# A gated recurrence on one core: the state in quarters of the columns by 32 of the batch, all products in 32-column tiles

## The chip, the core and the metric

The kernel runs on one core of a Trainium2 chip. The metric is the device time of one execution in microseconds (us), as the median of several runs. The core has TensorE (PE: products, with a separate weight load, PEld, before each), VectorE (DVE), ScalarE (ACT), GpSimd (POOL) and SyncE (SP, which issues most DMAs). Each engine works through its own queue in order, and semaphores tie the queues together. Products are written to PSUM, which has 128 partitions.

## What is computed

A gated recurrent unit over x of 64 sequences, 128 steps and 512 columns, all f32, with the input added to its output. The reference, cut to what matters:

```python
def step(h, inp):
    x_t, prop = inp
    comb = jnp.concatenate([x_t, h], axis=-1)
    z = jax.nn.sigmoid(comb @ Wz + bz)
    r = jax.nn.sigmoid(comb @ Wr + br)
    comb2 = jnp.concatenate([x_t, r * h], axis=-1)
    h_cand = jnp.tanh(comb2 @ Wh + bh)
    h_new = (1.0 - z) * h + z * h_cand
    h_next = jnp.where(prop, jnp.tanh(h_new @ Wp + bp), h_new)
    return (h_next, h_new)
# out = x + all h_new; prop is true at every fourth step but the last
```

Wz, Wr and Wh have 1024 rows: the first 512 meet x, the last 512 meet the state (or r * h). Wp has 512 rows. The order of the steps is forced; the products with x can be made ahead.

## The kernel before

**State.** `h`, `rh`, `z` and `keep` are tiles of 128 partitions by 256 columns (N): the 64 sequences (B) with the left half of the 512 columns lie on partitions 0 to 63, with the right half on 64 to 127.

**Products.** The transposed state is the weight of a product and a row block of W streams past it. `products` issues one call for each half of W's columns, with 64 columns of weight each; the output start (partition 0 or 64) puts the two into two 64-column tiles of TensorE. Each f32 call leaves two weight loads and two products in the trace (two passes). A gate is four such `products`, one for each 128 rows of W: 16 records of 128x256. All have line 225 in the profile.

**Turns.** The state must be transposed before it can be a weight. `turn` does 128 columns at a time on TensorE, as bf16 words against an identity (line 248, four records), and copies the result out of PSUM by VectorE or ScalarE (line 239). A state takes two `turn`s, eight records.

**A step** `t` (from line 677): the R gate on `hT`; sigmoid by ScalarE (line 751) and the product with h by VectorE (line 752), each in two halves of the columns; most of the Z gate, and in it the turns of `rh`; the two sigmoids of Z (lines 775, 776) and `keep` (line 777); the H gate on `rhT`; tanh (line 808), multiply (line 809) and add (line 814) in two halves; the turns of `h`, the first copied by VectorE, the second by ScalarE. In every fourth step ("Wp step") another gate with Wp, tanh (line 836) and turns of `hprop` follow. `seed` (line 410) copies the part of a gate that comes from x into PSUM before the products add the rest.

**The products with x.** For the first four and the last two steps they are plain. For all others, groups of four steps are done by a scheme with fewer multiplications: sums of blocks of x (GpSimd), sums of blocks of W (once), 192-column products into four PSUM banks `scratch_q`, `_r`, `_a`, `_x`, and sums back (`end_1`, `end_2`, lines 539 to 550: copies by ScalarE, adds by VectorE; then GpSimd, lines 580 and 584) into `cp`, from which `seed` reads. A unit of this work is one `products` call, four records. `batches` lists 98 units for eight steps; they stand in a list `queue`, and `fill(n)` puts the next n units where a step says. `read_out` issues the `end_` group of units that have been placed. How many go where is written out by hand in `PLACES`, three counts for each of eight steps, and in `TAIL` for the last nine. So TensorE's order is fixed in the program. x arrives twice, as `xr` (state layout, for the final sum) and as `xs` (for the transposed x, which VectorE makes with its own transpose, line 281).

Before the first step, `idle` issues products of zeros.

Of the kernel before, what the change touches and what calls it, by code (L numbers as in the profile page):

```python
# [17 lines left out]
def kernel(  # L18
# [14 lines left out]

# [5 lines left out]
    N = H // S  # L53
    C = N // P
# [6 lines left out]
    assert B * S == P and D == H and T % 8 == 0  # L61
# [10 lines left out]
    zeros = one.tile([P, 2 * N], BF16, tag="cq", name="zeros")  # L72
    nc.vector.memset(zeros, 0.0)
    ident = const.tile([P, P], F32, name="ident")
    make_identity(nc, ident)
    ones = const.tile([1, B], F32, name="ones")
    nc.gpsimd.memset(ones, 1.0)
    ident16 = const.tile([P, P], BF16, name="ident16")
    nc.vector.tensor_copy(ident16, ident)

# [5 lines left out]
    tw = {n: const.tile([P, S, S, 3, P], F32, name=f"tw_{n}") for n in (2, 3, 4)}  # L86
    tt = const.tile([P, 7, 3, S, 3, P // 2], F32, name="tt")
# [5 lines left out]
    def load_x(tile_, t0, n, j=0):  # L93
        for s in range(S):
            nc.sync.dma_start(
                out=tile_[s * B : (s + 1) * B, j : j + n, :], in_=x[:, t0 : t0 + n, ts(s, N)]
            )

    def load_w(wt, w, k0, k1, eng):
        eng.dma_start(  # L100
            out=wt[:, k0:k1, :],
            in_=w[k0 * P : k1 * P, :].rearrange("(k p) n -> p k n", p=P),
        )

    ORDER = [s * C + c for c in range(C) for s in range(S)]
    xr = {}

    def new_xr(g):
        xr[g] = xrp.tile([P, Q4, N], F32, tag="xr", name=f"xr_{g}")

    h_init = two.tile([P, N], F32, tag="h", name="h_init")
    bias_in = const.tile([P, 4, N], F32, name="bias")
    new_xr(0)
    for s in range(S):
        (nc.sync, nc.scalar)[s].dma_start(  # L115
            out=xr[0][s * B : (s + 1) * B, 0:2, :], in_=x[:, 0:2, ts(s, N)]
        )
    for k in ORDER:
        load_w(wx[:, :, R, :], Wr, k, k + 1, nc.sync)
    for i in (Z, H_):  # L120
        for k in (0, 2):
            load_w(wx[:, :, i, :], gates_in[i], k, k + 2, nc.sync)

    def load_bias(i, eng):
        for s in range(S):
            eng.dma_start(
                out=bias_in[s * B : (s + 1) * B, i, :],
                in_=(br, bz, bh, bp)[i][ts(s, N)]
                .rearrange("(o n) -> o n", o=1)
                .broadcast_to([B, N]),  # L130
            )
# [6 lines left out]
    for s in range(S):  # L138
        nc.gpsimd.dma_start(out=h_init[s * B : (s + 1) * B, :], in_=h0[:, ts(s, N)])
    for i in range(3):  # L140
        for k in (0, 2):
            load_w(wh[i], gates_in[i][D:, :], k, k + 2, nc.sync)
        if i == 0:
            load_x(xr[0], 2, 2, 2)
# [4 lines left out]

    xs = {}  # L150

    def load_xs(g):
        if g * Q4 < T:
            xs[g] = one.tile([P, Q4, S * C, 2, 32], F32, tag=f"xs{g % 2}", name=f"xs_{g}")
            for r in range(4):
                for bh in range(2):
                    nc.sync.dma_start(  # L157
                        out=xs[g][ts(r, 32), :, :, bh, :].rearrange("p t k e -> p (t k) e"),
                        in_=x[ts(bh, 32), g * Q4 : (g + 1) * Q4, :].rearrange(
                            "b t (k r e) -> r b (t k) e", k=S * C, r=4  # L160
                        )[r],
                    )

    load_xs(1)
    load_xs(2)
    load_w(wp, Wp, 0, 4, nc.sync)
    load_bias(3, nc.sync)
    new_xr(1)
    load_x(xr[1], 4, 4)


    rc = ps_c.tile([P, 2, N], F32, name="rc")
    zp = ps_c.tile([P, 2, N], F32, name="zp")
    slots = (rc[:, 0, :], zp[:, 0, :], rc[:, 1, :])
    slot_p = zp[:, 1, :]
    scratch = [ps_c.tile([P, 2 * N], F32, name=f"scratch_{n}") for n in "qrax"]
    q_ps, r_ps, a_ps, x_ps = (
        s[:, : 6 * P // 2].rearrange("p (m g u) -> p m g u", m=2, g=3) for s in scratch
    )


    turn_ps = [ps_c.tile([P, 2 * N], F32, name=f"turn_{c}") for c in range(C)]
    act_ps = [ps[:, N : N + P] for ps in turn_ps]

# [3 lines left out]
    def cut(ps):  # L188
        return ps.rearrange("p (c n) -> p c n", c=C)

    def spread(bank, rows, which):

        bank = bank.rearrange("p (i n) -> p i n", i=2)
        n = len(which)
        for s in range(S):
            nc.tensor.matmul(
                bank[s * B : (s + 1) * B, 0:n, :],
                lhsT=ones,
                rhs=bias_row[:, rows, ts(s, N)],
                start=True,  # L200
                stop=True,
            )
        for j, i in enumerate(which):
            nc.scalar.copy(bias_in[:, i, :], bank[:, j, :])

    bias0 = bias[:, 0, 0:3, :]
    bias_d = const.tile([P, 3, P], F32, name="bias_d")


    def idle(n):  # L210
        for i in range(n):
            s = i % S
            nc.tensor.matmul(
                (rc, zp)[i // S % 2][s * B : (s + 1) * B, :, :],
                lhsT=zeros[:, :B],
                rhs=zeros,
                start=True,
                stop=True,
            )


    def products(ps, lhs, rhs, start=False):

        for s in range(S):
            nc.tensor.matmul(  # L225
                ps[s * B : (s + 1) * B],
                lhsT=lhs,
                rhs=rhs(s),
# [4 lines left out]

    def product(ps, lT, w, k, start=False):
        s0, c0 = divmod(k, C)
        products(ps, lT[:, c0, ts(s0, B)], lambda s: w[:, k, ts(s, N)], start)

    def copy(eng, dst, src):
        (eng.copy if eng is nc.scalar else eng.tensor_copy)(dst, src)  # L239

    def turn(src, dst, c, name, eng):


        pt = turn_ps[c][:, :P].bitcast(BF16).rearrange("p (w n) -> p w n", w=2)
        for s in range(S):
            words = src[:, c * P + s * B : c * P + (s + 1) * B].bitcast(BF16)
            for w in range(2):
                nc.tensor.transpose(  # L248
                    pt[s * B : (s + 1) * B, w, :],
                    words.rearrange("p (n w) -> p w n", w=2)[:, w, :],  # L250
                    ident16,
                )
        copy(
            eng,
            dst[:, c, :].bitcast(U16).rearrange("p (n w) -> p n w", w=2),
            pt.bitcast(U16).rearrange("p w n -> p n w"),
        )

    def new_T(tag, name):
        return two.tile([P, C, P], F32, tag=tag, name=name)  # L260

# [3 lines left out]
    def new_xT(g):  # L265
        if g not in xT:
            xT[g] = xtp.tile([P, Q4, C, P], F32, tag="xT", name=f"xT_{g}")

    def turn_x(t, eng=nc.scalar):
        g, i = divmod(t, Q4)  # L270
        new_xT(g)
        src = xr[g]
        for c in range(C):
            turn(src[:, i, :], xT[g][:, i], c, f"xT_{t}", eng)

    def join_x(g, i):

        if g * Q4 >= T:
            return
        new_xT(g)  # L280
        nc.vector.transpose(  # L281
            out=xT[g][:, i].rearrange("p c (s b) -> p s c b", s=S),
            in_=xs[g][:, i].rearrange("p (s c) h e -> p s c (h e)", s=S),
        )


    def outer(kb, nb, ka):

        return wx[:, ka * C + kb, :, :].rearrange("p g (s n u) -> p n s g u", s=S, n=C)[:, nb]

# [11 lines left out]
    def inner(i, ka, na):  # L302
        return OPERAND[i](ka)[:, :, :, ts(na, P // 2)]

    def factor(i, j):

# [27 lines left out]

# [67 lines left out]
    def new_cp(q):  # L402
        if q not in cp:
            cp[q] = one.tile([P, C, 2, 3, P], F32, tag=f"cp{q % 2}", name=f"cp_{q}")
# [3 lines left out]
    def seed(i, t):  # L408
        if t < T:
            nc.scalar.copy(cut(slots[i]), G[t][:, :, i, :])  # L410

# [14 lines left out]

    def plain(t):

        first, second = scratch[:2] if t % 2 == 0 else scratch[2:]
        regions = (first[:, :N], first[:, N:], second[:, :N])  # L430
        g, i = divmod(t, Q4)

        def end():
            new_cp(t // 2)
            nc.vector.tensor_add(  # L435
                G[t][:, :, 0:2, :],
                first.rearrange("p (g c n) -> p c g n", g=2, c=C),
                bias[:, :, 0:2, :],
            )
            nc.vector.tensor_add(G[t][:, :, 2, :], cut(second[:, :N]), bias[:, :, 2, :])  # L440


        order = [(e, k) for e in range(3) for k in ORDER]
        if t == Q4 - 1:
            order = [(e, k) for k in ORDER for e in range(3)]
        units = [
            lambda e=e, k=k: product(
                regions[e], xT[g][:, i], wx[:, :, e, :], k, k == ORDER[0] and e != Z
# [3 lines left out]
        return [(u, None) for u in units[:-1]] + [(units[-1], end)]  # L452

    def plain_last():


        def banks(t):
            return scratch[:2] if t % 2 == 0 else scratch[2:]

        def units(t, gates, ks):  # L460
            first, second = banks(t)
            regions = (first[:, :N], first[:, N:], second[:, :N])
            return [
                lambda e=e, k=k: product(
                    regions[e], xT[LAST][:, t % Q4], wx[:, :, e, :], k, k == 3 and e != Z
# [5 lines left out]
        def end(t, gates):  # L471
# [485 lines left out]
```

## Time and profile before

| what | value |
|---|---|
| time, median of 3 runs | 1329.24 us (1328.91 to 1330.4) |
| profiled execution, first to last instruction | 1328.5 us, 37,727 instructions |
| mean granted TensorE clock | 0.999 |
| TensorE products / weight loads | 1319.2 us (99%) / 1117.0 us (84%), 15,312 each |
| VectorE / ScalarE / GpSimd | 57% / 42% / 66% |
| DMA | 62.22 MB, 171,438 packets, 133,600 of them under 512 bytes |

The profile is of one execution of its own; its time is given as the span in the second row, and nothing around that span is recorded. In a group's row stand the line, engine, operation, output<-input by name, shapes and count, then busy time and mean duration in ns, then idle time before it and what ended that. Durations of products overlap, so their count times their mean is more than their busy time; what they cost is read from start to start.

### The profile page before, as it was taken

What the parts mean: (1) busy time and instruction counts of PE and PEld (TensorE: products, weight loads), DVE (VectorE), ACT (ScalarE), POOL (GpSimd) and SP (SyncE); (2) the same over time, 40 slices, a digit from 0 to 9 for tenths busy, and PEclk for the clock granted to TensorE, in tenths of its full rate; (3) what the DMA queues carried; (4) which work ended last, traced back from release to release, by engine and by line L of the source; (5) the groups of instructions that cost most, each with busy time, mean ns of one, the idle gap of its engine ahead of it and who ended that gap; (6) DMA issues with size and microseconds to landing.
All of it is one profiled execution on the core that took longest, in us unless ns stands there. A gap on an engine that the chain in (4) does not pass through costs nothing.

```text
span 1328.5 us, 37727 instructions
## 1 busy us (share of the span) xinstructions
PE 1319.2 (99%) x15312; PEld 1117.0 (84%) x15312; DVE 750.8 (57%) x2000; ACT 554.4 (42%) x1733; POOL 881.5 (66%) x1032
## 2 busy tenths in 40 slices
PE   9999999999999999999999999999999999999998
PEld 5888888888888888888888888888888888888865
DVE  3655555555555555555555555555555555555544
ACT  1344444444444444444444444444444444444433
POOL 4876766766767577675777757676676676757530
PEclk9999999999999999999999999999999999999999
DMA  8421122121121221222111221212212112121030
GB/s 236 90 50 30 21 49 49 33 49 34 33 49 33 54 45 18 49 43 56 33 33 34 50 49 34 47 20 49 49 34 49 34 33 49 33 49 33 18 104 17
DMA packets 171438, 62.22 MB, mean 47 GB/s; under 512 B 133600, under 2 KB 166496, under 8 KB 171264
## 3 DMA queue, kind: packets, MB, share of 16 engines
q1 hardware_dynamic: 170880, 59.47, 20.8%
q8 instruction: 121, 1.98, 0.6%
q14 instruction: 53, 0.43, 0.1%
q10 hardware_dynamic: 224, 0.20, 0.1%
q0 software_dynamic: 160, 0.14, 0.0%
HBM read 43.00 MB, written 16.78 MB: 45 GB/s over the span
## 4 chain that ended last, share of the span: by engine, by line
PE 96%; SPq 1%; DMA 1%; DVE 0%; issue 0%; ACT 0%; DVEq 0%; ACTq 0%
PE rc L225 33%; PE zp L225 20%; PE scratch_q L225 11%; PE scratch_r L225 11%; PE scratch_x L225 11%; PE scratch_a L225 5%; PE turn L248 5%; DMA xr<-in_x_dram 1%; SPq L157 1%; SPq L100 0%; DMA bias<-in_L_cond_bp_dram 0%; DVE wx L333 0%; DVE turn L809 0%; SPq L115 0%; DVE xT L281 0%
## 5 line engine op out<-in xcount | busy, mean ns | idle before, releaser
L225 PE MATMUL rc<-wh,rhT 128*64 128x256 f32 x2048 | 246.0, 379 | 0.0
L580 POOL TENSOR_TENSOR cp<-mb,mb 128x768 f32<-128x768 f32 x75 | 136.3, 1818 | 107.4 <-ACT rc L410 47.5
L225 PE MATMUL zp<-wh,hT 128*64 128x256 f32 x1536 | 204.6, 379 | 0.0
L225 PEld LDWEIGHTS rc<-wh,rhT 128*64 128x64 f32 x2048 | 168.6, 137 | 40.1
L225 PE MATMUL rc<-wh,hT 128*64 128x256 f32 x1536 | 186.5, 383 | 0.4
L891 POOL TENSOR_TENSOR xr<-xr,h 128x256 f32<-128x256 f32 x127 | 92.7, 730 | 126.3 <-DVE h L814 126.3
L225 PEld LDWEIGHTS rc<-wh,hT 128*64 128x64 f32 x1536 | 122.3, 137 | 36.1 <-issue 10.1
L580 POOL TENSOR_TENSOR cp<-mb 128x768 f32<-128x768 f32 x47 | 85.3, 1815 | 94.7 <-DVE h L814 89.8
L225 PEld LDWEIGHTS zp<-wh,hT 128*64 128x64 f32 x1536 | 119.7, 137 | 24.7
L809 DVE TENSOR_TENSOR turn<-turn,z 128x128 f32<-128x128 f32 x256 | 75.4, 295 | 102.2 <-ACT turn L808 100.7
L239 DVE COPY rhT<-turn 128x256 uint16<-128x256 uint16 x256 | 97.6, 420 | 56.0 <-PE turn L248 51.6
L751 ACT ACTIVATE turn<-rc 128x128 f32<-128x128 f32 x256 | 55.3, 260 | 171.4 <-issue 113.8
L239 ACT COPY hT<-turn 128x256 uint16<-128x256 uint16 x127 | 47.3, 373 | 165.5 <-DVE hT L239 130.7
L548 DVE TENSOR_TENSOR mb<-scratch_r,cq 128x384 f32<-128x384 f32 (+1 forms) x107 | 59.3, 554 | 91.8 <-ACT cq L547 90.3
L580 POOL TENSOR_TENSOR mb<-mb,mb 128x768 f32<-128x768 f32 x58 | 105.4, 1817 | 8.5 <-DVE mb L550 8.5
L541 DVE TENSOR_TENSOR cx<-scratch_r,cx 128x384 f32<-128x384 f32 (+1 forms) x107 | 59.3, 554 | 88.0 <-ACT cx L539 88.0
L775 ACT ACTIVATE z<-zp 128x256 f32<-128x256 f32 x128 | 49.2, 384 | 136.7 <-PE zp L225 136.7
L410 ACT COPY rc<-cp 128x256 f32<-128x256 f32 x256 | 96.4, 377 | 18.3 <-DVE cp L435 4.6
L808 ACT ACTIVATE turn<-rc 128x128 f32<-128x128 f32 x256 | 55.2, 260 | 112.8 <-PE rc L225 111.7
L814 DVE TENSOR_TENSOR h<-turn,keep 128x128 f32<-128x128 f32 x254 | 74.1, 292 | 15.2
L248 PEld LDWEIGHTS <-h 128*64 128x64 bf16 x1016 | 68.1, 110 | 12.2 <-DVE h L814 6.5
L248 PE MATMUL turn<-ident,h 128*64 128x128 bf16 x1016 | 77.8, 220 | 0.3 <-DVE h L814 0.3
(165 smaller groups left out, 2931.7 us busy)
## 6 DMA issues: line engine op xcount, KB each, us to landing
xs<-in_x_dram SPq DMA_DIRECT2D x248, 64.0 KB, 2.8
xr<-in_x_dram SPq DMA_DIRECT2D x62, 256.0 KB, 4.1
out_dram<-xr SPq DMA_DIRECT2D x62, 256.0 KB, 3.3
wx<-in_L_cond_Wr_dram SPq DMA_DIRECT2D x7, 256.0 KB, 4.5
wx<-in_L_cond_Wz_dram SPq DMA_DIRECT2D x2, 512.0 KB, 6.4
wx<-in_L_cond_Wh_dram SPq DMA_DIRECT2D x2, 512.0 KB, 9.5
wh<-in_L_cond_Wr_dram SPq DMA_DIRECT2D x2, 512.0 KB, 12.7
wh<-in_L_cond_Wz_dram SPq DMA_DIRECT2D x2, 512.0 KB, 13.0
```

The lines of the kernel that those rows point to most:

```text
L225: nc.tensor.matmul(ps[s * B : (s + 1) * B], lhsT=lhs, rhs=rhs(s), start=start, stop=True, skip_group_check=True,)
L239: (eng.copy if eng is nc.scalar else eng.tensor_copy)(dst, src)
L248: nc.tensor.transpose(pt[s * B : (s + 1) * B, w, :], words.rearrange("p (n w) -> p w n", w=2)[:, w, :], ident16,)
L410: nc.scalar.copy(cut(slots[i]), G[t][:, :, i, :])
L541: nc.vector.tensor_add(T2[n][:, :nm], r_ps[:, :nm], T2[n][:, :nm])
L548: nc.vector.tensor_add(blocks()[:, :nm, 0, 1], r_ps[:, :nm], q2[:, :nm])
L580: nc.gpsimd.tensor_add(dst, a, b)
L751: nc.scalar.activation(act_ps[c], slots[R][:, ts(c, P)], AF.Sigmoid)
L808: nc.scalar.activation(pc, slots[H_][:, ts(c, P)], AF.Tanh)
L809: nc.vector.tensor_mul(pc, pc, z[:, ts(c, P)])
L814: nc.vector.tensor_add(h_new[:, ts(c, P)], pc, keep[:, ts(c, P)])
L891: nc.gpsimd.tensor_add(xr[g][:, j, :], xr[g][:, j, :], h_new)
```

## The change

The state is cut once more: quarters of the columns (J = 128) by 32 sequences (V). Partitions 32q to 32q+31 hold quarter q for one half of the batch, and the two halves of the batch lie side by side in the free dimension, [128, 2, 128]. With this layout the transpose that a product needs is one of 32x32 squares, which VectorE does in one instruction for a half. `product` and `products` now issue one call for each quarter of W's columns and each half of the batch: weights of 32 columns in four tiles, streams of 128 columns in a gate and of 96 in the batches.

```diff
+    def turn(dst, src):
+        nc.vector.transpose(out=dst, in_=src)
     def products(ps, lhs, rhs, start=False):
-        for s in range(S):
+        for q in range(NQ):
             nc.tensor.matmul(
-                ps[s * B : (s + 1) * B],
+                ps[part(q)],
                 lhsT=lhs,
-                rhs=rhs(s),
+                rhs=rhs(q),
...
+    def gate(i, lT, w):
+        for h in range(S):
+            for k in range(K):
+                products(
+                    pair(i)[:, h, :], lT[:, h, ts(k, V)], lambda q: w[:, k, ts(q, J)]
+                )
```

A step is now two chains, one for each half of the batch. The turns stand in VectorE's queue right behind what makes the state, and none stands in TensorE's:

```diff
+        gate(R, hT, wh[R])
...
+        for half in range(S):
+            r = pair(R)[:, half, :]
+            nc.scalar.activation(r, r, AF.Sigmoid)
+            nc.vector.tensor_mul(rh[:, half, :], r, h[:, half, :])
+            turn(rhT[:, half, :], rh[:, half, :])
...
+        gate(Z, hT, wh[Z])
...
+        fill(places[0])
+        gate(H_, rhT, wh[H_])
         read_out()
...
+        for half in range(S):
+            c = pair(H_)[:, half, :]
+            nc.scalar.activation(c, c, AF.Tanh)
+            nc.vector.tensor_mul(c, c, z[:, half, :])
...
+            nc.vector.tensor_add(h_new[:, half, :], c, keep[:, half, :])
+            turn(hT[:, half, :], h_new[:, half, :])
...
+        fill(places[1])
...
         if prop:
+            gate(P_, hT, wp)
             read_out()
+            for half in range(S):
+                nc.scalar.activation(h[:, half, :], pair(P_)[:, half, :], AF.Tanh)
+                turn(hT[:, half, :], h[:, half, :])
+            fill(places[2])
```

The hand-written places follow, 98 units for eight steps as before; the Wp steps are the first and the fifth of a row:

```diff
     PLACES = (
-        (6, 8, 6), (1, 7), (6, 6), (1, 7), (6, 8, 6), (1, 7), (1, 7), (6, 8),
+        (8, 3, 0), (3, 8, 0), (6, 8, 0), (6, 8, 0), (6, 4, 0), (4, 6, 0), (8, 6, 0), (8, 6, 0),
     )
```

Besides: the four PSUM banks `rc`, `zp` and `turn_0/1` become one tile `rec` of four banks, in which the two halves of R, of H and of the Wp gate lie in two different banks and Z in one; the x part, the sums of blocks and the batch products go to the same layout, with operands of the same number of elements for GpSimd, ScalarE and VectorE; x comes in eight transfers for each group and use, in rows of 512 bytes, and the outputs leave in eight for four steps (before: two and eight in, two out); the transposed x of the first eight steps is made from `xr`, so one `xs` load falls away; the weights come in transfers of 256 KB; the last output of each half leaves as soon as it is made, one on SP's queue and one on ScalarE's; `idle` issues 64, 16 and 32 products where it issued 16, 4 and 8; some of GpSimd's sums move by a step.

## The prediction

> **What bounds the kernel now.** I read the busy line of the page first, then the chain that ended last, then equal stretches, then TensorE in order of time, then groups by shape.
>
> ```profile
> PE 1319.2 (99%) x15312; PEld 1117.0 (84%) x15312; DVE 750.8 (57%) x2000; ACT 554.4 (42%) x1733; POOL 881.5 (66%) x1032
> PEclk9999999999999999999999999999999999999999
> PE 96%; SPq 1%; DMA 1%; DVE 0%; issue 0%; ACT 0%; DVEq 0%; ACTq 0%
> ```
>
> TensorE is busy 99% at the full granted clock, and the chain is 96% TensorE. A busy TensorE need not be a saturated one, so I looked at how its products stand in time. Two stretches of eight steps each:
>
> ```profile
> core 0: us, PE busy (x) PEld busy (x) DVE busy (x) ACT busy (x) POOL busy (x), PEclk, DMA share, GB/s
> 132.17:213.38 81.21, 81.21 (x954) 70.15 (x953) 46.92 (x125) 34.95 (x111) 56.21 (x67) 1.00 0.19 41
> 213.38:294.59 81.21, 81.21 (x955) 70.11 (x954) 46.92 (x125) 34.95 (x111) 56.24 (x67) 1.00 0.20 41
> ```
>
> The period is 81.21 us twice, without a hole. One step of it, columns start, length, engine, line, count:
>
> ```profile
> 133.76 1.49 PE L225 MATMUL zp<-wh,hT 128*64 128x256 f32 x12
> 135.05 0.42 PE L248 MATMUL turn<-ident,rh 128*64 128x128 bf16 x8
> 135.28 0.63 PE L225 MATMUL zp<-wh,hT 128*64 128x256 f32 x4
> 135.71 0.52 PE L225 MATMUL scratch_x<-tt,o 128*64 128x192 f32 x4
> 136.04 1.93 PE L225 MATMUL rc<-wh,rhT 128*64 128x256 f32 x16
> 137.76 0.53 PE L225 MATMUL scratch_x<-tt,o 128*64 128x192 f32 x4
> ```
>
> Start to start, 16 records of a gate take 1.72 us (107.8 ns each), four of a batch unit 0.325 (81.2 ns), eight turns 0.23. One 256-column record lasts 379 ns and a 192-column one 326 (groups by shape), so a column streams in 53/64 = 0.83 ns and 256 columns in 213. Two therefore always stream side by side, one per 64-column tile, and a pair costs 213 + 2.3 ns; a batch pair 160 + 2.4. TensorE is stream-bound: only what leaves its queue, or a change in how many stream at once, moves the time.
>
> **The change, part by part.**
>
> *The turns leave TensorE.* Each turn of a state is 8 records, 0.22 us. There are 291 of them (128 of rh, 127 of h, 31 of hprop, 5 at the start): 2,328 records at 27.6 ns, **-64 us**. All lie on the bound.
>
> *Products in 32-column tiles.* A product call issued 2 tiles x 2 passes; now 2 halves x 4 tiles x 2 passes, four times the records, each half as wide. If four tiles stream side by side as two do now, a gate round of four 128-column records is 107 + 2.3 = 109.0 ns and a batch round (96 columns) 80 + 2.4 = 82.4. The fixed 2.3 is taken per round, since two tiles and 128-column turns (eight in 0.22 us, 55 to 56 per pair against 53 of stream) show the same one. Gates and plain products are 6,928 records now (415 gates of 16, six plain steps of 48) and become 6,928 rounds: 6,928 x (109.0 - 107.8) = +8 us. Batches are 6,020 (15,312 less these, the turns and 36 others): 6,020 x (82.4 - 81.2) = +7 us, **+15 us** together. This holds only if TensorE starts a weight load and a product every 27 ns in a gate and every 20.6 ns in a batch, without end. The fastest row of the trace is the turns, 27.6 ns per load and product, and only eight long. So the cost of the tiles lies between +15 us and the price in the first rival; I take the low end, because nothing in the turns' row says that they were held by issue: their stream alone explains it.
>
> *The turns arrive on VectorE.* Rows:
>
> ```profile
> L239 DVE COPY rhT<-turn 128x256 uint16<-128x256 uint16 x256 | 97.6, 420 | 56.0 <-PE turn L248 51.6
> L281 DVE STREAM_TRANSPOSE xT<-xs 128x256 f32<-128x256 f32 x124 | 53.7, 436 | 1.9 <-issue 0.3
> L239 ACT COPY hT<-turn 128x256 uint16<-128x256 uint16 x127 | 47.3, 373 | 165.5 <-DVE hT L239 130.7
> L814 DVE TENSOR_TENSOR h<-turn,keep 128x128 f32<-128x128 f32 x254 | 74.1, 292 | 15.2
> ```
>
> A 128x128 square turn is not shown; it costs between half of 436 (218 ns) and all of it. I take 303: 436 less 128 elements at the 1.04 ns by which the elementwise rows grow (292 at 128, 425 at 256, `keep`). Per period VectorE loses 26 copies (16 rhT, 8 hT, 2 hpT; 10.9 us) and gains 36 turns (10.9 us): 46.9 of 81.2 stays as it is. ScalarE loses ten copies of 373. POOL's operations keep their sizes.
>
> *The two chains.* From the end of H's first half: drain and semaphore 0.20 us (ScalarE's sigmoid starts 0.415 us after the last product of its gate does, 0.213 of it stream), tanh 0.26, multiply, add and turn at 0.32 each with gaps, 0.1 to the load: 1.6 us. The halves share VectorE; the second half is ready about 1.65 us after H's end. R's first half (0.87 us) covers part, so 0.8 us of other products must stand between H and R, 2.4 units of 0.33. The bias-and-sum groups (`end_1`, `end_2`) are queued ahead of that chain where a batch part ends in the first place of a step. `end_2` is one copy of 486 and three adds of 550 and pushes the multiply back by 1.1 us; `end_1` by 0.45. The needs are then 1.9 and 1.25 us. The new places give 8 units (2.6 us) or 6 almost everywhere, but in the two steps of a period with Wp, 3 (1.0 us, after `end_1`) and 4 (1.3 us, after `end_2`): holes of 0.25 and 0.55 us. Behind Wp no unit is left: tanh, turn and the semaphore (0.9 us) against its second half (0.87), 0.05 each. With the R gate's starts (holes of 0.02 to 0.04 now) about 1.0 us per period of TensorE waiting, **+15 us** over some 15 periods. Bounds: 0, if these groups finish sooner, and 40, if turns cost 436 and every H gate waits 0.2 more. R to H is covered by Z (1.75 us) and the first place.
>
> *Start, end, DMA.* At the start eight x transfers instead of two stand before Wr (SP takes 0.63 to 0.76 us for one), and the idle matmuls grow from 28 to 112, which makes 28 rounds for 14: I take **+2 us** (bounds -2 and +5), because the first 40 us run at a DMA share of 0.88 and most of the delay meets the weights' arrival. SP issues 24 transfers in four steps instead of 12, at 0.49 to 0.63 us some 14 of 40 us; xs rows grow from 128 to 512 bytes, so the data engines have less to do. Two steps before the end eight stores stand on SP ahead of the last one, 5 us against a last step of 6: nothing, or +3 if they slip.
>
> Sum against the profiled span: 1328.5 - 64 + 15 + 15 + 2 = 1296.5. The timed median, 1329.24, is 0.7 above that span: **1297 us**. The low end is without holes: 1328.5 - 64 + 2 + 0.7 = 1267, rounds at no extra cost.
>
> The margin is thin: 32 us over 12,948 rounds, so 2.5 ns more per round, or 5.3 per batch round alone, and it is gone.
>
> The Trainium skill speaks against the change here. Its page "TensorE: Matmul & The Clock Gate", section on why the gap is 56 and not 53.3 ns, says that products never start less than about 25 ns apart, however small. Four of those would make a batch round 100 ns, and the sum by that rule about 1297 + 6,020 x 17.6 ns = 1403, an estimate from that page. The same page, part on packing small matmuls, has products in different tiles starting 4 ns apart, by which my sum stands. The trace cannot choose: its records of two tiles lie as close as 7 ns, but only in pairs.
>
> **Rivals.**
>
> 1. *Issue or weight loading becomes TensorE's bound* (slower). For it: a load is now needed per 128 or 96 columns, and the weight-load row is already 84%. A 64-column f32 load lasts 137 ns against 110 for bf16, so its columns take 0.83 ns too: 27 ns for 32 columns, 107 for four if they go one after another, over a batch round's 80. The turns' 27.6 ns gives 110. Either way a gate round stays near 110, a batch round rises by 28 ns: 6,020 x 28 + 6,928 x 1.4 = +178, and the holes fill (-15): 1460 us. Against it: the turns' two loads of a pair fit under their own stream. It decides from 5.3 ns per batch round.
>
> 2. *Only two tiles stream at once*, as in every row now (slower). Rounds double: 6,928 x 109 + 6,020 x 82.4 more, 1250 us: about 2540 us. Against it: nothing in the pairs marks two as a limit, since only two tiles exist.
>
> 3. *The chains set the end.* TensorE has no turns left to wait for, but both turns of h are now VectorE's. With holes of 2.5 to 3.5 us per period, 1320 to 1335 us: most or all of the gain gone. For it: places of 3 and 4 units in the Wp steps. Against it: VectorE is 57% busy and stays there.
>
> **How the numbers follow.** Main case (1267 to 1312) 0.55; rival 3, 0.10 (half faster, 0.03 same, 0.02 slower); rival 1, 0.28, spread from 1335 to 1460; rival 2, 0.07. About 0.2% (2.7 us) is what a measurement of this kernel tells from no change. Faster 0.60, same 0.03, slower 0.37. The range runs from 1267 to rival 1's 1460 and leaves out rival 2 and the tails; the main case's own is 1267 to 1312.
>
> **What would show it.** L248's turns gone from TensorE; some 51,800 products of 128*32, with 128 or 96 columns at about 272 and 246 ns; 64 of a gate in 1.75 us and 16 of a unit in 0.33. If 16 take 0.44, it is rival 1; 0.66, rival 2. A period of 79 us rather than 81.2, with TensorE waiting on VectorE's turns in the two Wp steps only, would confirm the holes; many such waits mean rival 3. VectorE turns of 128x128 near 303 ns, some 574 of them. I am wrong if a gate's 64 need over 1.8 us.

## The result, and the profile after

The changed kernel takes 1786.18 us (median of 4 runs, 1784.62 to 1789.36) against 1329.74 us for the one before on the same chip: a ratio of 1.3439, 95% interval [1.342, 1.3458]. The forecast was 1297 us, with a range of 1267 to 1460. The page of after, its busy line, the granted clock, the instruction queue and the chain that ended last:

```profile
PE 1378.8 (77%) x51920; PEld 1273.5 (71%) x51920; DVE 786.7 (44%) x2163; ACT 529.6 (30%) x1571; POOL 884.0 (49%) x1030
...
PEclk7799999999999999999999999999999999999999
...
q8 instruction: 406, 6.65, 1.5%
...
PE 64%; DVE 14%; ACT 11%; issue 5%; SPq 3%; DMA 2%; POOL 1%; ACTq 0%; DVEq 0%; POOLq 0%
```

TensorE was 99% busy and is now 77% busy; 36% of the chain is something else. Whatever went wrong, it is not the speed of a product. The order of time, TensorE alone (start, length, engine, line, count, and in brackets the idle time just ahead and what ended it), shows both at once:

```profile
803.27 1.93 PE L200 MATMUL rec<-wh,rhT 128*32 128x128 f32 x64
805.02 0.51 PE L200 MATMUL scratch_a<-tw,xT 128*32 128x96 f32 x16
805.35 0.51 PE L200 MATMUL scratch_a<-wx,xT 128*32 128x96 f32 x16
...
808.13 1.93 PE L200 MATMUL rec<-wh,hT 128*32 128x128 f32 x64
811.91 1.96 PE L200 MATMUL rec<-wh,hT 128*32 128x128 f32 x64 [1.85 <-ACT rec L364]
...
820.47 1.74 PE L200 MATMUL rec<-wp,hT 128*32 128x128 f32 x56 [1.21 <-ACT rec L364]
```

A gate's 64 records need 1.75 us (803.27 to 805.02), a unit's 16 need 0.33 (805.02 to 805.35): four tiles do stream side by side, as forecast. But Z (811.91) starts 1.85 us after R has ended, released by ScalarE's line 364, which is `seed`, the copy of the *next* step's x part. TensorE's waits for that copy come to 302 us in the whole kernel, those for VectorE's turned `hprop` to 27 (in total, times, longest):

```profile
PE rec L200 <- ACT rec L364: 302.2, 215, 2.1
PE rec L200 <- DVE hpT L227: 26.9, 30, 0.9
```

Before, Z followed R without a gap: R's 16 records, below, start 1.75 us ahead of the Z at 133.76 that the prediction shows.

```profile
132.01 1.95 PE L225 MATMUL rc<-wh,hT 128*64 128x256 f32 x16
```

Two stretches of after, columns as in the prediction's table of stretches:

```profile
0.00:63.50 63.50, 36.95 (x648) 23.68 (x652) 5.57 (x16) 4.23 (x12) 12.94 (x21) 0.69 0.28 99
135.60:243.30 107.70, 84.23 (x3292) 78.73 (x3288) 48.94 (x134) 33.58 (x99) 59.10 (x72) 1.00 0.15 38
```

Until the first sigmoid of Z 63.4 us pass (before: 26.0), at a DMA share of 0.28. Eight steps (from one such sigmoid to the same eight steps on) take 107.7 us, 107.1 on average, where they took 81.21.

Three theories, which may all hold. **T, one tile:** `rec` joined four PSUM banks under one name, and the waits go by the tile: a gate waits until ScalarE and VectorE have finished with another gate that lies in another bank. **S, supply:** there are 3.4 times the instructions for TensorE (51,920 pairs of load and product for 15,312), and they do not come fast enough. **D, loads:** the weights' transfers have a shape that keeps most DMA engines idle. In the expectations A and B stand for what each says there.

### The profile page after: what moved, and what is told of

Read it like the earlier page. It is cut to its first block, busy times and chain, and to the rows that moved or that the text cites. A ratio compares the mean times of both kernels' runs of the same rounds, so it can differ in the third digit from the quotient of the medians.

```text
span 1787.6 us, 111363 instructions
## 1 busy us (share of the span) xinstructions
PE 1378.8 (77%) x51920; PEld 1273.5 (71%) x51920; DVE 786.7 (44%) x2163; ACT 529.6 (30%) x1571; POOL 884.0 (49%) x1030
## 3 DMA queue, kind: packets, MB, share of 16 engines
q8 instruction: 406, 6.65, 1.5%
## 4 chain that ended last, share of the span: by engine, by line
PE 64%; DVE 14%; ACT 11%; issue 5%; SPq 3%; DMA 2%; POOL 1%; ACTq 0%; DVEq 0%; POOLq 0%
PE rec L200 44%; PE scratch_x L200 5%; PE scratch_r L200 5%; PE scratch_q L200 5%; ACT rec L364 5%; DVE rh L659 4%; PE scratch_a L200 4%; SPq L93 2%; DVE rec L704 2%; DVE h L713 2%; DVE rhT L227 2%; ACT rec L658 2%; DVE keep L672 1%; DVE hT L227 1%; ACT rec L703 1%
## 5 line engine op out<-in xcount | busy, mean ns | idle before, releaser
L200 PE MATMUL rec<-wh,hT 128*32 128x128 f32 x12288 | 393.1, 278 | 200.3 <-ACT rec L364 187.9
L200 PEld LDWEIGHTS rec<-wh,hT 128*32 128x32 f32 x12288 | 337.3, 111 | 241.4 <-ACT rec L364 221.5
L200 PE MATMUL rec<-wh,rhT 128*32 128x128 f32 x8192 | 255.7, 274 | 33.0 <-ACT rec L364 22.6
L200 PEld LDWEIGHTS rec<-wh,rhT 128*32 128x32 f32 x8192 | 224.4, 110 | 46.7 <-ACT rec L364 29.7
L364 ACT COPY rec<-cp 128x256 f32<-128x256 f32 x384 | 144.6, 377 | 218.4 <-DVE h L713 87.1
L200 PE MATMUL rec<-wh,hpT 128*32 128x128 f32 x3968 | 121.5, 274 | 82.3 <-ACT rec L364 55.3
L200 PEld LDWEIGHTS rec<-wh,hpT 128*32 128x32 f32 x3968 | 105.4, 110 | 98.2 <-ACT rec L364 63.7
L703 ACT ACTIVATE rec<-rec 128x128 f32<-128x128 f32 x256 | 67.1, 262 | 311.7 <-PE rec L200 217.3
L658 ACT ACTIVATE rec<-rec 128x128 f32<-128x128 f32 x256 | 67.1, 262 | 302.1 <-PE rec L200 256.4
L704 DVE TENSOR_TENSOR rec<-rec,z 128x128 f32<-128x128 f32 x256 | 76.7, 300 | 114.8 <-ACT rec L703 114.8
L466 ACT COPY cq<-scratch_q 128x384 f32<-128x384 f32 (+1 forms) x214 | 101.4, 474 | 22.5 <-PE scratch_q L200 22.1
L475 DVE TENSOR_TENSOR cx<-scratch_r,cx 128x384 f32<-128x384 f32 (+1 forms) x107 | 59.3, 554 | 98.1 <-ACT cx L466 98.1
L510 POOL TENSOR_TENSOR cp<-mb 128x768 f32<-128x768 f32 x47 | 85.9, 1827 | 12.3 <-ACT rec L364 10.9
```

The costliest lines, as they stand in the source:

```text
L200: nc.tensor.matmul(ps[part(q)], lhsT=lhs, rhs=rhs(q), start=start, stop=True, skip_group_check=True,)
L364: nc.scalar.copy(halves(pair(i)), G[t][:, :, :, i, :].rearrange("p c h n -> p h c n"))
L466: nc.scalar.copy(c[:, :nm], ps[:, :nm])
L475: nc.vector.tensor_add(T2[n][:, :nm], r_ps[:, :nm], T2[n][:, :nm])
L510: nc.gpsimd.tensor_add(dst, a, b)
L658: nc.scalar.activation(r, r, AF.Sigmoid)
```

## Experiments: the waits of one tile

**e1_late_seed.** The seed that ended Z's wait is moved behind Z.

```diff
-        if t != 3:
-            seed(R, t + 1)
...
+        seed(R, t + 1)
         seed(Z, t + 1)
```

> The changed kernel with one statement moved: the copy that seeds the next step's R gate (line 364, called behind the R sigmoids) is issued behind the Z sigmoids instead. Nothing else differs. Theory A (the four PSUM banks of rec are one tile, so the Z gate is ordered behind the R seed though they share no element): TensorE's 1.9 us wait before each Z gate goes, 128 x 1.9 = 243 us less, about 1545 us, and the H gate inherits at most a few tenths. Theory B (the chain through ScalarE and VectorE is simply too long for the units placed, whatever the tile): the wait moves to the H or the next R gate and the time stays within 30 us of 1786.

1769.61 us, ratio 1.3313 [1.3289, 1.3338]. TensorE's longest waits of this kernel (in total, times, longest):

```profile
PE rec L200 <- DVE rh L659: 173.3, 126, 1.6
PE rec L200 <- ACT rec L364: 85.5, 91, 2.1
```

The seed is gone as Z's releaser and VectorE's `rh` has its place: the product of R and h, which reads another bank of the same tile. With the last user taken away, the one ahead of it ends the wait. The time lies within the 30 us of B, but the wait did not move to H or R, as B has it: Z still waits. My expectation took one user for the cause; the cause is that there are several.

**e2_own_tiles** and **e4_halves** cut the tile itself: into R with Wp (two banks), H and Z; and into four one-bank tiles, each half of R with the same half of Wp, then Z with H's first half, and H's second half.

```diff
-    rec = ps_c.tile([P, 4, 4 * J], F32, name="rec")
+    ps_a = ps_c.tile([P, 4 * J], F32, name="ps_a")
+    ps_b = ps_c.tile([P, 4 * J], F32, name="ps_b")
+    ps_z = ps_c.tile([P, 4 * J], F32, name="ps_z")
+    ps_h = ps_c.tile([P, 4 * J], F32, name="ps_h")
```

> The changed kernel with rec cut into three PSUM tiles: two banks for R and Wp, one for H, one for Z (both halves of H then lie in one bank). Order, places and instructions are the same. Theory A: no wait before Z, seeds of one gate no longer hold another; the waits of one half for the other inside a gate stay (tanh of Wp's first half waits for its whole gate, about 1.0 us before R in the Wp steps). Eight steps go from 107 to 87 to 90 us, the whole to about 1490 us (1450 to 1550). Theory B: 1760 or more.

> The changed kernel with four one-bank PSUM tiles, so that the halves of R, of Wp and of H lie in different tiles (H's first half shares one with Z); a seed becomes two copies, one per half, except for Z. Theory A: the two chains are really two, the waits of e2 inside a gate go as well; eight steps take 79 to 83 us, the whole about 1375 us (1350 to 1410), 37 of the excess over 1329 being the start. Theory B: 1700 or more.

e2: 1611.15 us, ratio 1.2122 [1.2104, 1.214], 97.1 us per eight steps. e4: 1602.15, ratio 1.2054 [1.2034, 1.2074], 95.8 us. So 184 us come back with the cut of the tile alone (1786.2 - 1602.2). But both miss theory A's range: e2 takes 7 us per eight steps or more beyond it, e4 13 or more. What is left has another releaser; TensorE's waits of e4_halves:

```profile
PE ps_z L208 <- issue: 30.1, 53, 1.3
PE scratch_q L208 <- issue: 27.2, 47, 1.3
PE scratch_r L208 <- issue: 25.2, 51, 1.4
PE scratch_x L208 <- issue: 22.6, 42, 1.2
PE ps_a L208 <- issue: 22.2, 26, 1.4
```

"issue" means that nothing the profile shows was waited for. And the holes fall in the middle of gates and units alike.

**e11_before_one_tile** does the harmful part alone, in the kernel before:

```diff
-    rc = ps_c.tile([P, 2, N], F32, name="rc")
-    zp = ps_c.tile([P, 2, N], F32, name="zp")
+    rec = ps_c.tile([P, 2, 2, N], F32, name="rec")
+    rc, zp = rec[:, 0], rec[:, 1]
```

> The kernel before with its two PSUM tiles rc (gates R and H) and zp (Z and Wp) made one tile of two banks; nothing else changes. A, a tile is tracked as a whole: each gate now waits until ScalarE and VectorE have read and written the gate ahead of it, as in the kernel after, where the hole from R to Z was 1.89 us, the one from a batch to Wp 1.48 and from Wp to R 1.17: 8 x 1.89 + 2 x 1.48 + 2 x 1.17 = 20.4 us in eight steps at most, 8 to 20 us by how much of it the batches' units hide: 1450 to 1640 us. B, banks are tracked (the holes of the kernel after have another cause): within 5 us of 1329.

1603.41 us, ratio 1.2062 [1.2044, 1.208]; 98.1 us per eight steps for 81.2. TensorE in order of time, and the wait:

```profile
803.82 1.95 PE L225 MATMUL rec<-wh,hT 128*64 128x256 f32 x16
806.80 1.52 PE L225 MATMUL rec<-wh,hT 128*64 128x256 f32 x12 [1.03 <-ACT rec L410]
```
```profile
PE rec L225 <- ACT rec L410: 215.0, 191, 1.7
```

The same hole from R to Z, with the same releaser (line 410 is `seed` there). A line that declares memory costs this kernel 274 us. T is shown from both sides.

## Experiments: the start

**e3_load.** In after, one 256 KB transfer takes a row block of each of the four quarters. Now one takes all rows of a quarter, in 32 partitions; bytes and number are the same.

```diff
-            out=wt[:, k, :],
-            in_=w.rearrange("(q k e) n -> k q e n", q=NQ, k=K)[k],
+            out=wt[part(q), :, :],
+            in_=w[q * P : (q + 1) * P, :].rearrange("(k e) n -> e k n", k=K),
```

> The changed kernel with only the weights' loads cut the other way: one transfer for each quarter of the partitions (32 partitions of four rows) instead of one for each k (four groups of 32 partitions); bytes and count of transfers are the same. Theory A for the start (the transfers' shape spreads over too few data engines: a share of 0.28 at 99 GB/s in the first 63 us, where before it was 0.88 at 241): the first z appears near 28 us instead of 63.5, and 33 to 37 us go: 1749 to 1755 us. Theory B for the start (eight x transfers ahead of the weights, and SP's issue time, delay it): under 8 us gained.

The first sigmoid of Z comes at 36.7 us in place of 63.4. The stretch up to it:

```profile
0.00:36.80 36.80, 28.45 (x654) 20.49 (x658) 5.57 (x16) 4.24 (x12) 12.98 (x21) 0.91 0.86 193
```

The DMA share is 0.86 for 0.28, at 193 GB/s for 99. In after, four packets of the main queue were under way at once for 70% of that stretch; here sixteen or more for 59%. D holds for the start. But the time is 1778.06 us, ratio 1.3379 [1.3359, 1.3399]: 8 us less, not 27, because eight steps took 108.3 us instead of 107.1. **e5_halves_load** joins it to e4_halves:

> Both cures together: four PSUM tiles of one bank each (as in e4_halves, 1602.2 us) and the loads of the weights with one transfer for each quarter of the partitions (as in e3_load). A, supply of instructions: after the start a period of eight steps still needs 6464 instructions of TensorE, 25.25 blocks of 256 at the 3.75 us between the transfers of two blocks that e4_halves showed, 94.7 us; only the start gains, 8 to 27 us: 1575 to 1594 us, periods still 94 to 98 us. B, what is left of the periods came from the late start or from waits that go with it: under 1500 us, periods under 88 us.

1574.24 us, ratio 1.1831 [1.1806, 1.1855], 28 us under e4_halves, at the lower edge of A, with 95.9 us per eight steps as before. There the start's gain came through.

## Experiments: the supply of instructions

The instruction queue moves blocks of 16 KB (after: 6.65 MB in 406 packets). The Trainium skill, "Runtime: NRT & Kernel Launch", section "Instruction fetch mechanics", says what these are: 256 instructions each, fetched in sequence ahead of execution, and hidden because an engine issues more slowly than blocks come. The count agrees (e4_halves: 104,173 records of TensorE, 407 blocks, 256 each); that the fetch is hidden does not. I numbered all of TensorE's records (loads, products and semaphore instructions; without the last the places blur) and added up the time from start to start by the place in a block of 256, in sixteenths, over the steady part (200 us to 85% of the span):

| kernel | the other sixteenths, ns | the 13th, ns | a block, us | holes over 0.3 us, of these in the 13th |
|---|---|---|---|---|
| before | 644 to 709 | 697 | 10.80 | none |
| after | 239 to 282 | 383 | 4.23 | 265, 73 |
| e4_halves | 190 to 215 | 833 | 3.79 | 273, 257 |
| e5_halves_load | 191 to 217 | 829 | 3.78 | 276, 261 |
| e6_before_cut4 | 231 to 233 | 366 | 3.84 | 51, 51 |
| e7_before_cut2 | 364 to 381 | 375 | 5.94 | none |
| e8_joined_rz | 224 to 249 | 404 | 3.86 | 84, 73 |
| e9_mixed | 249 to 306 | 285 | 4.50 | 182, 15 |

In e5_halves_load 261 of 276 holes begin at one and the same place of 256, whatever product stands there. No semaphore of the program knows of such a place. The surplus, 829 - 195 = 0.63 us a block, makes 16 us in eight steps (25.25 blocks): what separates 95.9 from 80. The records of the instruction queue show what ends them. At these holes the last transfer had begun some 147 records earlier (90 to 171), and TensorE goes on 2.5 us after that start (2.25 to 2.9). Transfers last from 0.88 to 1.66 us, but the hole ends 1.40 us after the end of the transfer, with a standard deviation of only 0.10 us, and 1.38 to 1.41 us in e4_halves, e6_before_cut4 and e8_joined_rz. The next transfer begins 1.06 to 1.73 us after the hole. So TensorE runs dry when these records need less time than the one block on its way. No semaphore names this wait; the times do, and the kernels below test it.

**e6_before_cut4** and **e7_before_cut2** go the other way: the kernel before, same tiles and columns, with each stream cut in pieces.

```diff
+        for c in range(4):
             for s in range(S):
...
+                r, o = r[:, ts(c, u)], o[:, ts(c, u)]
```

> The kernel before with the stream of every product that is not a turn cut into four pieces (64 columns in a gate, 48 in the batches), each with its own weight load: same tiles of 64 columns, same columns streamed, 3432 pairs of load and product in eight steps in place of 954, so 6864 instructions. A, supply of instructions: 26.8 blocks of 256 at 3.75 us (3.28 at the shortest that was seen) make 100.5 us (88) in place of 81.2: 1630 us (1435 to 1650), with holes in TensorE's stream at one place of every block of 256 instructions. B, only the stream counts (2.6 ns for each further round, the rest 0.83 ns a column): 84.5 us, some 1380 us, no such holes. Unchanged at 1330 would say that neither counts.

> Control for e6_before_cut4: the stream of every product cut into two pieces (128 and 96 columns), 1780 pairs, 3560 instructions in eight steps. A, supply: 13.9 blocks at 3.75 us make 52 us, under the 81.2 us of the stream, so it does not bind: 1330 to 1350 us. B, a cost for each further instruction, whatever their rate: a third of what e6_before_cut4 adds.

e7: 1343.9 us, ratio 1.0113 [1.0098, 1.0128], no holes; its eight steps take 82.16 us, 0.95 more for some 404 further rounds of two tiles, 2.4 ns each (1,760 products for 952; the expectation counted 20 too many). e6: 1662.11 us, ratio 1.2502 [1.2472, 1.2531], 101.6 us per eight steps, near A's 100.5, and the time is just above A's range. The number came out for the wrong reason: the table has 231 ns in *every* sixteenth, 57.8 ns for a round of two pieces, against 366 in the 13th. The holes cost 134 ns a block, 3.6 us of the 20.4. The rest is even; the page has

```profile
PE 1610.9 (97%) x54156; PEld 1592.7 (96%) x54156; DVE 757.0 (46%) x2000; ACT 560.7 (34%) x1733; POOL 884.9 (54%) x1032
```

Weight loads are busy 96%: a load of 64 columns, 53 ns by the 0.83 ns a column of the prediction, now serves a stream of 48 or 64. That this is its bound is argued, not tested apart. e6 is therefore weak evidence for S.

**e8_joined_rz** takes instructions away and keeps the columns: R and Z share their weights, so one stream of 256 columns serves both.

```diff
+                products(
+                    ps_rz[h][:, : 2 * J].rearrange("p (i n) -> p i n", i=2),
+                    lT[h][:, ts(k, V)],
+                    lambda q: wh_rz[:, k, :, ts(q, J)],
+                )
```

> As e5_halves_load, but the R and the Z gate are one stream of 256 columns for each half of the batch (both use the same transposed state), with the transposed state in a tile for each half, and PSUM banks (R, Z) and (H, Wp) for each half. Columns streamed and weights of 32 columns in four tiles as before it; 5440 instructions in eight steps in place of 6464, and Z no longer stands behind the sigmoids of R. A, supply: 21.25 blocks at 3.75 us make 79.7 us, now about the length of the stream (78 us): periods of 79 to 86 us, 1330 to 1440 us. B, something else keeps the period at 95 us (the chain of a step, or a fixed cost in the four tiles): periods over 92 us, over 1540 us.

1381.16 us, ratio 1.0389 [1.0366, 1.0413]; 82.7 us per eight steps. 193 us went with 16% of the instructions. The 13th sixteenth keeps a surplus of 175 ns, 3.7 us in eight steps (21.25 blocks) where e5 had 16; the 12.3 us between them are about 190 us over 15.5 times eight steps, so the order of R and Z, changed in the same edit, explains little: in e5_halves_load TensorE's waits at Z's tile for a seed (line 377) are 7.5 us in all from 200 to 1340 us, and 9.7 us after that.

```profile
PE ps_z L212 <- ACT ps_z L377: 7.5, 15, 0.7
```

The rest, about 79 us in both, is stream. S is shown, and this table, not e6, shows it. TensorE's waits from 200 to 1200 us:

```profile
PE scratch_q L208 <- issue: 8.6, 18, 1.2
PE scratch_r L208 <- issue: 4.3, 11, 0.9
PE ps_a L208 <- issue: 3.9, 8, 1.2
PE scratch_x L208 <- issue: 3.8, 12, 0.6
```

No gate waits for ScalarE any more; what waits is units, where the records are densest.

**e9_mixed** therefore spread the short units among the long records (`fill(n[k])` behind each row block of the R-Z stream). e10, in spite of its label, is the same kernel again.

> As e8_joined_rz (1381.2 us, periods of 80.9 to 85.2 us, mean 82.6), with the same instructions in another order: all but two units of each batch's share are put between the four row blocks of the R-Z stream (after its first and its second half), not in one stretch. A, supply counts by the block: in e8_joined_rz a block of 256 instructions that holds only units and an H gate streams in 2.6 to 3.1 us, less than the 3.28 to 3.75 us that the next block takes to come, while one of the R-Z stream lasts 7 us; mixed, every block streams in 3.1 to 4 us: periods of 79.5 to 81.5 us, 1335 to 1365 us. B, only the mean rate counts (21.25 blocks at 3.8 us): unchanged, 1373 to 1388 us. C, the R chain is delayed by the units ahead of it and sets the period: over 1390 us.

> The kernel of e9_mixed once more, for its spread alone: within 6 us of it.

1563.5 us, ratio 1.1759 [1.1737, 1.1781], and once more 1560.52. C was right. The holes have left the 13th sixteenth, so the spreading does what A says of the blocks, but the kernel pays far more elsewhere (TensorE, 200 to 1200 us):

```profile
PE ps_a L208 <- DVE hT L242: 80.0, 63, 1.8
PE scratch_x L208 <- ACT cx L490: 27.0, 33, 0.9
PE ps_z L208 <- ACT ps_z L717: 22.4, 20, 1.1
```

The units were the cover of the chain; inside the R-Z stream they are on it.

**e12_light_mix** left two there.

> As e8_joined_rz (1381.2 us), with three changes of order and no other: only two units of the batches go between the row blocks of the second half of the R-Z stream, none into the first; the sigmoids of its first half come ahead of the read-out of a batch in the program; and x of steps 2 and 3 is loaded behind the weights of the state. A, the holes of e9_mixed came from the length of the chain (it put four units into each half of the R-Z stream and left two for the cover): with most units back as cover the holes at H go, those at the blocks of 256 shrink (2 us of a period in e8_joined_rz), and the start gains up to 7 us: 1345 to 1378 us. B, any unit inside the R-Z stream lengthens the chain that sets the period: over 1390 us.

1426.79 us, ratio 1.0734 [1.0716, 1.0752]: the time that B gives, though not by the chain. The new wait is

```profile
PE scratch_x L208 <- ACT cx L490: 27.7, 36, 1.1
```

A unit among R-Z now waits for the read-out of the batch before it. Probably my own second change, the sigmoids first, put that read-out later: e9_mixed has the same order and the same wait. No run tests it alone. The first sigmoid of Z came at 36.9 us (37.5 in e8), so loading x later gained almost nothing. No version here beats the kernel before; e8_joined_rz comes nearest.

## Why the prediction was wrong, point by point

From after back: own tiles -184.0 us, loads -27.9, a sixth fewer instructions -193.1, and e8_joined_rz is still 51.9 us above before. Of the 46 us between their profiled spans (1374.5 and 1328.5) 18 are the start, 21 are fourteen stretches of eight steps that take 1.5 us more each, and 7 are the last twelve steps.

- *Turns leave TensorE, -64:* right, no turn is left among TensorE's records. VectorE's squares take 312 ns (forecast 303):

```profile
L227 DVE STREAM_TRANSPOSE rhT<-rh 128x128 f32<-128x128 f32 x256 | 79.8, 312 | 8.7
```

- *Rounds of four tiles, +15:* right as a rate, 109 ns for a gate's round (1.75 us for 16) and 82 for a batch's, products of 274 and 246 ns (forecast 272 and 246). Without the holes at the blocks, e5 and e8 would run at 79 to 80 us per eight steps (95.9 - 16 and 82.7 - 3.7), the forecast's 79. Its condition failed: "a weight load and a product every 27 ns in a gate and every 20.6 ns in a batch, without end". I priced the array and the weight loads, and looked for a limit in a row of eight records. The page of before had the instruction queue (`q8 instruction: 121, 1.98, 0.6%`: 121 packets for 15,312 pairs, 256 instructions each); 3.4 times as many is 406, which in 1297 us is one every 3.2 us, and I never asked how fast they can come. After's own blocks lose only some 0.13 us, probably since the waits at the gates give the fetch time; with the waits gone it is 0.63. So neither cure can be priced alone.
- *Chains, +15 with bounds 0 and 40:* the term that failed most. "R to H is covered by Z (1.75 us) and the first place" is true only if Z may start. The joining of four banks into `rec`, which the description of the change names, got no line in the sum. It costs 184 us in after and 274 in the kernel before. TensorE waited for VectorE's `hpT` 30 times and 26.9 us, 0.9 us each, where the sum has 0.05; in e4_halves, with Wp's halves in two tiles, that wait is gone.
- *Start, +2 with bounds -2 and 5:* Z's sigmoid of the fifth step comes at 135.6 us for 87.3, +48. I counted x's transfers and the idle products, and not the new shape of the weights' transfers (27 us of it). e8 keeps +18 with that shape mended.
- *Rivals:* the first named the right place, the rate at which TensorE gets its work, with the wrong mechanism: 16 records take 0.33 us, not 0.44, so four loads do not go one after another. Its 0.83 ns a column for a load was read from two rows that both have 64 columns (137 ns in f32, 110 in bf16), which do not give it; the f32 loads of 32 columns in after, 110 ns, do. The Trainium skill's page "TensorE: Matmul & The Clock Gate", section "Wait — 56ns, not 53.3ns?", has a floor of about 25 ns from start to start; four tiles start one product every 20.6 ns, so this trace does not keep it. Rival 2 (two tiles) is refuted by the same rows, and rival 3 was far too small and named the wrong places.

Open: why e3_load lost 19 of its 27 us. Its 13th sixteenth takes 431 ns for after's 383, 1.2 us in eight steps, which is the size of it, but no run says why.

## What to carry to other kernels

A declaration that puts several PSUM banks under one name makes one thing of them for every wait: look for each tile that a change joins, and ask who still reads or writes any part of it. Count instructions for each engine, not only work, when tiles get smaller: count the blocks that the instruction queue will have to move, and compare the time that a block takes to run with the time between two transfers in the densest stretch of a trace. Where two limits lie on top of each other, undoing one shows little; undo them together, and read by place, not only by sum, what is left.

## What the runs showed of the hardware

TensorE was fed a block of 256 instructions every 3.78 us at best over a long stretch (e4, e5), 14.8 ns an instruction; blocks that last 5.94 us on average (e7) showed no hole. Where it ran dry, it went on 1.4 us after the end of the block's transfer. Four 32-column tiles keep the column rate of two 64-column ones (a gate in 1.75 us for 1.72) and start products 20.6 ns apart on average. A transfer of 256 KB spread over all four quarters of the partitions held the start at 99 GB/s, the same bytes in 32 partitions each ran at 193.
